# Scan layer of a four-layer network: two projection copies and the first output half moved in the hand-written plan

## Chip, cores and metric

One Trainium2 chip, one core. The metric is the device time of one execution in microseconds (us). The kernel before takes 3412.58 us, the median of 3 runs (3409.98 to 3416.41).

## The reference, cut to what matters

Four layers, each added to its input; the last one is a selective scan over 2304 tokens of each of three images, and the change touches nothing else.

```python
xz = jnp.einsum('blc,dc->bld', xn, in_proj_w)            # 256 -> 512 + 512 channels
x_in, z = jnp.split(xz, 2, axis=-1)
xc = jax.lax.conv_general_dilated(xc, conv_w, ...)       # 4 taps along the tokens
u = jax.nn.silu(xc).transpose(0, 2, 1)
x_dbl = jnp.einsum('bld,ed->ble', u, x_proj_w)           # -> dt_raw, B_ssm, C_ssm
dt = jax.nn.softplus(jnp.einsum('blr,dr->bld', dt_raw, dt_proj_w) + dt_proj_b)
def step(hst, inp):                                      # 512 channels x 16 states
    dA = jnp.exp(dt_t[:, :, None] * A)
    hst = hst * dA + dt_t[:, :, None] * B_t[:, None, :] * u_t[:, :, None]
    y_t = jnp.einsum('bdn,bn->bd', hst, C_t)
y = ys.transpose(1, 0, 2) + u * D_param
y = y * jax.nn.silu(z)
out = jnp.einsum('bld,cd->blc', y, out_proj_w)
```

All data are float32.

## The kernel before, in words

**Stages.** The first three layers (an attention block and two 3x3 convolutions) fill the first 2018 us. Then the scan layer runs for some 1370 us. Its tokens are cut into 18 chunks of 384 (3 images by 6), and a chunk's 512 inner channels into four blocks of 128 (m = 0 to 3; the change's "tiles"). One chunk holds 64 scan instructions on VectorE: four blocks, two halves of the states (h), eight parts. Scan n of a chunk is part n mod 8 of step (m, h), with n = 16m + 8h + part.

**A scan's feed.** ScalarE computes the decays of each scan, exp(dt A), into one of three PSUM banks (`decay`, L1792), VectorE scans them (`scan`, L1800). The decay for scan n + 3 is put out right behind scan n, since it takes scan n's bank. The scan works in place on a tile `hs`, which VectorE and GpSimd have filled with dt B u (`fill`): GpSimd the lower half (L1766, and a quarter at L1762), VectorE the upper (`fill_upper`, L1748), which reads `ps_r`. That is a two-bank PSUM tile, the only one of its pool; `spread_pe` (L1717) has TensorE write a quarter of dt u into each bank, once for each block m, at the end of its forerunner's first half. For the first half of a block (h = 0) `fill_upper` reads both banks; for the second half it reads the first bank only. After a step GpSimd multiplies by C (`times_c`, L1817), TensorE sums the states (`add_states`, L1829 and L1834) and VectorE gates with silu(z) (`gate`, L1841).

**What sets the order.** All else in a chunk is squeezed between these scans by a plan that is written by hand. A chunk has 16 places j (four scans each, so j = 0 to 3 is block 0), and in each the points BEGIN, MID, DONE, LATE (behind the first, second, third and fourth scan and the decay that follows it) and PE_ (for TensorE). An entry (j, point, rel, stage) runs `stage` for the chunk `rel` away from the one being scanned: rel 1 prepares the next chunk, rel -1 finishes the one before. `run` goes through `after`, `plan`, `gating` and `last_of_all` in this order. `keep_order` pins the resulting order on TensorE, VectorE, ScalarE and GpSimd, and each engine takes its instructions one after another; DMAs go through SyncE's queue in the order in which they are written.

**The stages around the change.** `project_x` (L1263) writes a block's projection into `whole[m % 2]`, one of two shared PSUM banks (`bank` is a view of these). `take_x` (L1269) copies it to SBUF on ScalarE. `taps` (L1273) makes the convolution, 4 matmuls into `bank[m % 2]`. `take_u` (L1281) moves that to `u` on ScalarE with the bias. `silu` (L1286) is one Silu over a whole chunk with a table load ahead of it, and another behind it (L229) that brings back the table with Exp. `silu(k.sz)` at (3, LATE) is that of z; `silu(k.u)` at (7, LATE) that of u. `project_y(k, mo)` (L1361, L1363) is half mo of the output projection with the residual, in `bank[mo]`; `store` copies it on ScalarE (L1373) and issues the output's DMA (L1374). `residual` (L1370) loads `k.ot`. Blocks 2 and 3 of the next chunk go through j = 2 to 5, the output half 0 of the chunk before through j = 5 and 6.

Of the kernel before, what the change touches and what calls it, by code (L numbers as in the profile page):

```python
# [16 lines left out]
P = 128  # L17
# [8 lines left out]
CH = 384  # L26
# [9 lines left out]
DI = 4  # L36
# [48 lines left out]
def net(  # L85
# [21 lines left out]
    nc = tc.nc  # L107
# [14 lines left out]
    def v(name, i=0, n=1):  # L122
        at = VEC_AT[name] + i
        return vec[:, at : at + n]

    ident = const.tile([P, P], F32, name="ident")
# [6 lines left out]
        out=gview, in_=gview, pattern=[[-8, 16], [0, 8]], compare_op=ALU.is_ge,  # L133
# [3 lines left out]
        out=gview, in_=gview, pattern=[[8, 16], [0, 8]], compare_op=ALU.is_ge,  # L137
# [243 lines left out]
    with ExitStack() as l0:  # L381
# [17 lines left out]
        def w(name, at, n):  # L399
            a = W0_AT[name] + at  # L400
            if a < W0_SPLIT:
                return w0a[:, a : a + n]
            return w0b[:, a - W0_SPLIT : a - W0_SPLIT + n]
# [14 lines left out]
        with ExitStack() as p1:  # L418
# [15 lines left out]
            for b in ORDER:  # L434
# [23 lines left out]
                for c in range(NCH):  # L458
                    for m, dst in ((0, y1), (1, cur[b])):
                        pm = ps.tile([P, 512], F32, tag="s", name="ps_y")  # L460
                        for ct in range(CT):
                            nc.tensor.matmul(  # L462
                                pm[:, :CH], ws[:, ct, m * P : (m + 1) * P], chunk(xb[:, ct, :], c),
                                start=ct == 0, stop=ct == CT - 1,
# [70 lines left out]
        with ExitStack() as p2:  # L535
# [9 lines left out]
            for i in range(NB):  # L545
# [400 lines left out]
                for mt in range(0, NT, 2):  # L946
                    pv = pair()
                    for j in range(2):
                        nc.tensor.matmul(
                            pv[:, j, :384], cur[2][:, (mt + j) * P : (mt + j + 1) * P], wn[2],  # L950
                            start=True, stop=True,
# [158 lines left out]
    def room(k, name):  # L1110
        return rooms[name][k.at % len(rooms[name])]
# [87 lines left out]

    class Chunk:  # L1200
        def __init__(self):
            self.second = {}


    whole = [psg.tile([P, 512], F32, name=f"ps_g{j}") for j in range(2)]
    bank = [t[:, :CH] for t in whole]
# [54 lines left out]
    def project_x(k, m):  # L1261
        for ct in range(CT):
            nc.tensor.matmul(  # L1263
                whole[m % 2][:, :XH], w3v["winx"][:, ct, m * P : (m + 1) * P], k.xn[:, ct, :],
                start=ct == 0, stop=ct == CT - 1,
            )

    def take_x(k, m):
        nc.scalar.copy(w3v["xi"][:, m % 3, :], whole[m % 2][:, :XH])  # L1269

    def taps(k, m):
        for tap in range(DCONV):
            nc.tensor.matmul(  # L1273
                bank[m % 2], w3v["taps"][:, m, tap, :], w3v["xi"][:, m % 3, tap : tap + CH],
                start=tap == 0, stop=tap == DCONV - 1,
            )

    def take_u(k, m):
        if m == 0:
            k.u = room(k, "u")  # L1280
        nc.scalar.activation(  # L1281
            k.u[:, m, :], bank[m % 2], AF.Identity, bias=v("conv_b", m)
        )

    def silu(t):
        nc.scalar.activation(t, t, AF.Silu)  # L1286
        exp_ln_tables()
# [68 lines left out]
            k.sz = room(k, "sz")  # L1356
        nc.scalar.copy(k.sz[:, m, :], bank[j])

    def project_y(k, mo, lo=0, hi=DI):
        if lo == 0:  # L1360
            nc.tensor.matmul(bank[mo], ident, k.ot[:, mo, :], start=True, stop=False)  # L1361
        for m in range(lo, hi):
            nc.tensor.matmul(  # L1363
                bank[mo], w("out", m * 256 + mo * P, P), k.sz[:, m, :],
                start=False, stop=m == DI - 1,
            )

# [2 lines left out]
        nc.sync.dma_start(k.ot, xd[k.b][:, :, k.c * CH : (k.c + 1) * CH])  # L1370

    def store(k, mo):
        nc.scalar.copy(k.ot[:, mo, :], bank[mo])  # L1373
        nc.sync.dma_start(  # L1374
            out[k.b, mo * P : (mo + 1) * P, k.c * CH : (k.c + 1) * CH], k.ot[:, mo, :]
        )
# [3 lines left out]
    BEGIN, MID, DONE, LATE, PE_ = range(5)  # L1380
# [15 lines left out]
        (2, DONE, 1, lambda k: project_x(k, 2)),  # L1396
        (2, LATE, 1, lambda k: take_u(k, 1)),
        (2, LATE, 1, lambda k: project_x(k, 3)),
        (3, LATE, 1, lambda k: take_x(k, 2)),
        (3, LATE, 1, lambda k: taps(k, 2)),  # L1400
        (4, BEGIN, 1, lambda k: take_x(k, 3)),
        (4, BEGIN, 1, lambda k: taps(k, 3)),
        (4, DONE, 1, lambda k: take_u(k, 2)),
        (5, MID, 1, lambda k: take_u(k, 3)),
        (7, LATE, 1, lambda k: silu(k.u)),
        (8, BEGIN, 1, project_u),
        (8, LATE, 1, take_dbc),
# [11 lines left out]
        (0, MID, 0, lambda k: k.at and take_z(k, 2, 0)),  # L1419
        (0, MID, 0, lambda k: k.at and take_z(k, 3, 1)),  # L1420
        (2, MID, -1, residual),
        (5, BEGIN, -1, lambda k: project_y(k, 0)),
        (6, MID, -1, lambda k: store(k, 0)),
        (7, PE_, -1, lambda k: project_y(k, 1)),
        (8, MID, -1, lambda k: store(k, 1)),
    ]

    last_of_all = [(3, LATE, 0, lambda k: silu(k.sz))]

# [246 lines left out]
    with ExitStack() as l3:  # L1676
# [35 lines left out]
        def spread_pe(k, m):  # L1712

            t = psr.tile([P, 2, 512], F32, name="ps_r")
            for q in range(2):
                r = slice(32 * q, 32 * q + 32)
                nc.tensor.matmul(  # L1717
                    t[:, q, :CH], rep[r].rearrange("p r d -> p (r d)"), k.dtu[r, m, :],
                    start=True, stop=True,
                )  # L1720
            k.ps = t


        steps = [(at, m, h) for at in range(len(todo)) for m in range(DI) for h in range(2)]
# [120 lines left out]
        k = chunks[0]  # L1845
        k.rows = {0: spread(k, 0)}
        spread_second(k, 0)
        spread_pe(k, 0)
        first_states(0)
        fill(0)  # L1850
        for n in range(3):
            decay(n)
        for s, (at, m, h) in enumerate(steps):
# [35 lines left out]
            if h == 0 and s + 2 < len(steps):  # L1889
                spread_pe(chunks[steps[s + 2][0]], steps[s + 2][1])  # L1890

        end = len(steps) - 1
        k = chunks[last]
        residual(k)
        for mo in range(2):
            project_y(k, mo, 0, DI - 1)
        add_states(end)
        gate(*steps[end][:2])
        for mo in range(2):
            project_y(k, mo, DI - 1, DI)  # L1900
            store(k, mo)
# [29 lines left out]
def net_kernel(tc, *args):  # L1931

    with tc.tile_pool(name="flag", bufs=1) as pool:
        flag = pool.tile([1, 1], I32, name="flag")
        net(tc, *args, flag, False)
        bad = tc.nc.values_load(flag[:1, :1])
        with tc.If(bad > 0):
            net(tc, *args, None, True)
# [77 lines left out]
```

## Time and profile before

| | |
|---|---|
| median of 3 runs | 3412.58 us (3409.98 to 3416.41) |
| the profiled execution's own time | 3411.51 us |
| its span, first to last instruction | 3409.8 us |
| scans, first start to last end | 2018.1 to 3389.4 us |
| one chunk (first scan to first scan), in turn | 77.4 and 76.3 us |
| VectorE busy in two chunks of 77.40 and 76.30 us | 73.83 and 73.72 us |
| ScalarE busy in them | 62.80 and 62.80 us |
| GpSimd busy in them | 72.30 and 69.73 us |
| TensorE busy in them | 64.08 and 61.84 us |
| VectorE's waits for a decay, all scans | 45.8 us in 50 waits, longest 1.4 us |

How to read it: the page has the busy time of each engine, the span in 40 slices, the chain that ended last and the costliest groups. A line names the kernel's line, the engine, the operation, what it writes `<-` reads, the shape, and the count; then busy time, mean ns of one and the idle time of its engine just ahead of it, with what ended that idle time. PE is TensorE, DVE VectorE, ACT ScalarE, POOL GpSimd, SP SyncE; PEclk is the TensorE clock that was granted, 1.00 being full. A timeline has start, duration, and in brackets the idle time ahead with its releaser; `x3` joins three instructions without a break. Times in it count from the span's start.

### The profile page before, as it was taken

What the parts mean: (1) busy time and instruction counts of PE and PEld (TensorE: products, weight loads), DVE (VectorE), ACT (ScalarE), POOL (GpSimd) and SP (SyncE); (2) the same over time, 40 slices, a digit from 0 to 9 for tenths busy, and PEclk for the clock granted to TensorE, in tenths of its full rate; (3) what the DMA queues carried; (4) which work ended last, traced back from release to release, by engine and by line L of the source; (5) the groups of instructions that cost most, each with busy time, mean ns of one, the idle gap of its engine ahead of it and who ended that gap; (6) DMA issues with size and microseconds to landing.
All of it is one profiled execution on the core that took longest, in us unless ns stands there. A gap on an engine that the chain in (4) does not pass through costs nothing.

```text
span 3409.8 us, 52160 instructions
## 1 busy us (share of the span) xinstructions
PE 3047.4 (89%) x19882; PEld 1442.5 (42%) x19882; DVE 2902.4 (85%) x3302; ACT 2381.6 (70%) x3596; POOL 1335.5 (39%) x457
## 2 busy tenths in 40 slices
PE   7999999999999999979999987878888888878785
PEld 4334343453333435547677753333333333333331
DVE  3799889959989996479966369999999999999998
ACT  2688888848888885332233558888888888888874
POOL 0000000000000000210000039999899999999897
PEclk8999999999999999989999998888889898988887
DMA  4000000010000002756501144545555454545552
GB/s 167 28 8 10 8 8 7 12 42 5 8 10 8 7 8 80 238 171 222 199 22 38 42 116 110 120 115 139 141 126 131 121 122 121 128 114 136 137 133 54
DMA packets 182152, 290.65 MB, mean 85 GB/s; under 512 B 34737, under 2 KB 148465, under 8 KB 179970
## 3 DMA queue, kind: packets, MB, share of 16 engines
q1 hardware_dynamic: 168658, 267.15, 29.0%
q10 hardware_dynamic: 13232, 20.06, 1.8%
q8 instruction: 158, 2.59, 0.3%
q14 instruction: 104, 0.85, 0.1%
HBM read 236.24 MB, written 50.64 MB: 84 GB/s over the span
## 4 chain that ended last, share of the span: by engine, by line
PE 59%; DVE 21%; ACT 11%; DMA 4%; issue 3%; POOL 1%; SPq 1%; ACTq 0%; DVEq 0%; POOLq 0%
PE ps_s L638 16%; PE acc L651 14%; DVE hs L1800 13%; PE ps_c L1533 8%; PE ps_g L1273 3%; PE ps_g L1222 3%; ACT ps_da L1792 2%; DVE u L296 2%; PE ps_y L462 2%; PE ps_m L665 1%; PE ps_s L1031 1%; PE ps_m L711 1%; PE ps_y L1834 1%; PE ps_g L1349 1%; ACT L229 1%
## 5 line engine op out<-in xcount | busy, mean ns | idle before, releaser
L642 ACT ACTIVATE pt<-ps_s 128x1024 f32<-128x1024 f32 x972 | 942.6, 1022 | 154.5 <-PE ps_s L638 141.8
L1800 DVE TENSOR_TENSOR_SCAN hs<-ps_da,hs 128x385 f32<-128x385 f32 x1152 | 1006.6, 940 | 47.4 <-ACT ps_da L1792 45.8
L857 DVE TENSOR_TENSOR part<-part,pt 128x2048 f32<-128x2048 f32 x396 | 906.8, 2290 | 41.2 <-ACT pt L642 18.4
L1792 ACT ACTIVATE ps_da<-dtr,u 128x384 f32<-128x384 f32 x1152 | 657.0, 583 | 201.7 <-DVE hs L1800 191.0
L164 POOL TENSOR_TENSOR rstd<-ve,mhalf 128x2 f32<-128x2 f32 (+1 forms) x26 | 16.4, 631 | 1476.5 <-DVE ve L162 1476.5
L638 PE MATMUL ps_s<-q,kt 32*128 32x512 f32 (+1 forms) x4320 | 576.4, 592 | 0.1
L651 PE MATMUL acc<-pt,vt 128*32 128x512 f32 (+1 forms) x4320 | 520.9, 561 | 0.2
L1533 PE MATMUL ps_c<-vt,u 128*128 128x288 f32 x1728 | 432.5, 411 | 21.0 <-DVE u L263 21.0
L1817 POOL TENSOR_TENSOR hc<-hs,x 128x3072 f32<-128x3072 f32 x72 | 405.3, 5629 | 5.4 <-DVE hs L1800 5.2
L1817 POOL TENSOR_TENSOR hc<-hs,bc 128x3072 f32<-128x3072 f32 x71 | 399.8, 5631 | 11.0 <-DVE hs L1800 7.9
L1533 PEld LDWEIGHTS ps_c<-vt,u 128*128 128x128 f32 x1728 | 331.0, 192 | 117.6 <-issue 19.8
L638 PEld LDWEIGHTS ps_s<-q,kt 32*128 32x128 f32 x4320 | 195.3, 183 | 199.1 <-issue 120.2
L1834 PE MATMUL ps_y<-hc,u 128*32 128x384 f32 x2304 | 252.0, 562 | 17.3 <-POOL hc L1817 17.3
L651 PEld LDWEIGHTS acc<-pt,vt 128*32 128x32 f32 x4320 | 94.4, 108 | 353.4 <-issue 326.7
L1273 PE MATMUL ps_g<-u 128*128 128x384 f32 x576 | 199.5, 494 | 21.0 <-ACT u L1269 20.9
L1766 POOL TENSOR_TENSOR hs<-dtur,x 128x1536 f32<-128x1536 f32 x72 | 209.2, 2905 | 7.2 <-DMA dtur<-dtud 7.2
L1766 POOL TENSOR_TENSOR hs<-dtur,bc 128x1536 f32<-128x1536 f32 x72 | 209.6, 2911 | 0.0
L1318 PE MATMUL ps_g<-wconv,u 17*128 17x384 f32 x144 | 79.2, 684 | 106.7 <-ACT x L1339 81.0
L1273 PEld LDWEIGHTS ps_g<-u 128*128 128x128 f32 x576 | 107.0, 190 | 110.5 <-ACT u L1269 42.2
L1222 PE MATMUL ps_g<-wconv,u 128*128 128x384 f32 x144 | 85.6, 765 | 64.6 <-ACT x L1339 64.1
L1834 PEld LDWEIGHTS ps_y<-hc,u 128*32 128x32 f32 x2304 | 65.4, 119 | 178.8 <-issue 152.6
L1549 ACT COPY cb<-ps_c 128x288 f32<-128x288 f32 x48 | 19.2, 399 | 158.4 <-PE ps_c L1533 144.2
(251 smaller groups left out, 3842.5 us busy)
## 6 DMA issues: line engine op xcount, KB each, us to landing
wconv<-in_we SPq DMA_DIRECT2D x144, 384.0 KB, 4.2
dtr<-dtd SPq DMA_DIRECT2D x288, 192.0 KB, 4.0
dtur<-dtud SPq DMA_DIRECT2D x288, 96.0 KB, 4.2
wconv<-xd SPq DMA_DIRECT2D x36, 384.0 KB, 4.9
x<-bcd SPq DMA_DIRECT2D x72, 192.0 KB, 5.3
dtd<-x SPq DMA_DIRECT2D x36, 384.0 KB, 3.5
dtuq<-dtud SPq DMA_DIRECT2D x288, 48.0 KB, 2.2
bc<-bcd SPq DMA_DIRECT2D x72, 192.0 KB, 5.1
```

What stands on the lines that cost most here:

```text
L638: nc.tensor.matmul(s[:, j, cols], kt[r, mt * P : (mt + 1) * P], q[r, :n], start=True, stop=True,)
L642: nc.scalar.activation(p[:, h0 : h0 + 2, :], s, AF.Exp)
L651: nc.tensor.matmul(acc[h * HD : (h + 1) * HD, :n], vt[:, mt, g * P + h * HD : g * P + (h + 1) * HD], p[:, h, cols], start=mt == 0, stop=mt ...
L857: ): nc.vector.tensor_tensor(part, first, p, ALU.add)
L1222: nc.tensor.matmul(bank[to], w3v["less"][:, int(to != ct), :], k.xg[:, ct, :], start=ct == 0, stop=ct == CT - 1,)
L1273: nc.tensor.matmul(bank[m % 2], w3v["taps"][:, m, tap, :], w3v["xi"][:, m % 3, tap : tap + CH], start=tap == 0, stop=tap == DCONV - 1,)
L1533: nc.tensor.matmul(pc[:, :HN], u[:, i, dy, ct, m * P : (m + 1) * P], vt[:, i, ct, dy * TW : dy * TW + HN], start=ct == 0 and dy == 0, stop ...
L1766: nc.gpsimd.tensor_tensor(states(s)[:, :, 2:4, 1:], chunks[at].rows[m][1].unsqueeze(1).broadcast_to([P, 2, 2, CH]), b_rows(s, 0, 2), ALU.mult,
L1792: nc.scalar.activation(slots[n % 3][:, 1 : CH + 1], chunks[at].rows[m][0][:, q, :], AF.Exp, scale=amat[:, col : col + 1],)
L1800: nc.vector.tensor_tensor_scan(b, slots[(8 * s + part) % 3][:, : CH + 1], b, 0.0, ALU.mult, ALU.add)
L1817: nc.gpsimd.tensor_tensor(hc, tiles[s][:, :, :, 1:], cb.broadcast_to([P, 2, 4, CH]), ALU.mult)
L1834: nc.tensor.matmul(k.y_ps[32 * q : 32 * q + 32, :CH], fold, hc[:, g, q, :], start=False, stop=h == 1 and g == 1,)
```

## The change

Blocks 2 and 3 are taken later: `take_x` and `taps` of block 2 go from (3, LATE) to (4, BEGIN), those of block 3 from (4, BEGIN) to (4, DONE); `take_u` from (4, DONE) and (5, MID) to (5, LATE) and (6, LATE). Output half 0 goes from (5, BEGIN) to (4, BEGIN), its `store` from (6, MID) to (5, DONE). So that it needs no shared bank there, it is summed in the second bank of `ps_r`, which `spread_pe` leaves in `lent`. The number of instructions of each engine is the same.

```diff
         def __init__(self):
-            self.second = {}
+            self.second, self.y_out = {}, {}
...
-    def project_y(k, mo, lo=0, hi=DI):
+    def project_y(k, mo, lo=0, hi=DI, into=None):
         if lo == 0:
-            nc.tensor.matmul(bank[mo], ident, k.ot[:, mo, :], start=True, stop=False)
+            k.y_out[mo] = bank[mo] if into is None else into
+            nc.tensor.matmul(k.y_out[mo], ident, k.ot[:, mo, :], start=True, stop=False)
         for m in range(lo, hi):
             nc.tensor.matmul(
-                bank[mo], w("out", m * 256 + mo * P, P), k.sz[:, m, :],
+                k.y_out[mo], w("out", m * 256 + mo * P, P), k.sz[:, m, :],
                 start=False, stop=m == DI - 1,
             )
...
     def store(k, mo):
-        nc.scalar.copy(k.ot[:, mo, :], bank[mo])
+        nc.scalar.copy(k.ot[:, mo, :], k.y_out[mo])
...
-        (3, LATE, 1, lambda k: take_x(k, 2)),
-        (3, LATE, 1, lambda k: taps(k, 2)),
-        (4, BEGIN, 1, lambda k: take_x(k, 3)),
-        (4, BEGIN, 1, lambda k: taps(k, 3)),
-        (4, DONE, 1, lambda k: take_u(k, 2)),
-        (5, MID, 1, lambda k: take_u(k, 3)),
+        (4, BEGIN, 1, lambda k: take_x(k, 2)),
+        (4, BEGIN, 1, lambda k: taps(k, 2)),
+        (4, DONE, 1, lambda k: take_x(k, 3)),
+        (4, DONE, 1, lambda k: taps(k, 3)),
+        (5, LATE, 1, lambda k: take_u(k, 2)),
+        (6, LATE, 1, lambda k: take_u(k, 3)),
...
-        (5, BEGIN, -1, lambda k: project_y(k, 0)),
-        (6, MID, -1, lambda k: store(k, 0)),
+        (4, BEGIN, -1, lambda k: project_y(k, 0, 0, DI, lent[0])),
+        (5, DONE, -1, lambda k: store(k, 0)),
...
+    lent = [None]
...
             k.ps = t
+            lent[0] = t[:, 1, :CH]
```

## The prediction

> **What bounds the kernel now.** I read the page's groups first: the scans are VectorE's largest group, they come one after another over 1371 us, and little idle time stands ahead of them.
>
> ```profile
> L1800 DVE TENSOR_TENSOR_SCAN hs<-ps_da,hs 128x385 f32<-128x385 f32 x1152 | 1006.6, 940 | 47.4 <-ACT ps_da L1792 45.8
> ```
>
> So VectorE bounds the scan layer, and time can be won only where it waits. The view of waits, for VectorE over the scan layer, has one entry of weight, the same 45.8 us:
>
> ```profile
> DVE hs L1800 <- ACT ps_da L1792: 45.8, 50, 1.4
> ```
>
> Sorted by the scan that waits, this is 17 waits at scan 19 of a chunk (18.7 us; 1.13 us in most chunks), 16 at scan 59 (14.0 us; 1.37 and about 0.35 us in turn), 16 at scan 61 (12.2 us) and one more. The change lies around scan 19. The timeline of ScalarE in the chunk that starts at 2480.70 shows how that wait arises:
>
> ```profile
> 2494.90 0.59 ACT L1792 ACTIVATE ps_da<-dtr,u 128x384 f32<-128x384 f32 x1 [0.27 <-DVE hs L1800]
> 2496.22 0.48 ACT L1269 COPY u<-ps_g 128x387 f32<-128x387 f32 x1 [0.74 <-PE ps_g L1263]
> 2496.72 1.28 ACT L1286 ACT_TABLE_LOAD   x1
> ...
> 2500.92 0.58 ACT L1792 ACTIVATE ps_da<-dtr,u 128x384 f32<-128x384 f32 x1
> 2501.44 0.47 ACT L1269 COPY u<-ps_g 128x387 f32<-128x387 f32 x1
> ```
>
> After the decay for scan 18, ScalarE idles 0.74 us for TensorE's projection of block 2, copies it, and only then starts z's Silu. The decay for scan 19 starts at 2500.92. VectorE in the same stretch (the scan's second line is scan 19):
>
> ```profile
> 2494.77 0.54 DVE L1841 TENSOR_TENSOR sz<-ps_y,sz 128x384 f32<-128x384 f32 x1
> ...
> 2497.75 2.66 DVE L1800 TENSOR_TENSOR_SCAN hs<-ps_da,hs 128x385 f32<-128x385 f32 x3
> 2501.53 4.47 DVE L1800 TENSOR_TENSOR_SCAN hs<-ps_da,hs 128x385 f32<-128x385 f32 x5 [1.13 <-ACT ps_da L1792]
> 2505.92 0.54 DVE L1748 TENSOR_TENSOR hs<-ps_r,x 128x384 f32<-128x384 f32 x1
> 2506.37 1.80 DVE L1800 TENSOR_TENSOR_SCAN hs<-ps_da,hs 128x385 f32<-128x385 f32 x2
> ```
>
> The last chunk has no next one to prepare, so it has z's Silu without the copies. ScalarE there, then VectorE:
>
> ```profile
> 3337.86 1.28 ACT L1286 ACT_TABLE_LOAD   x1
> ...
> 3341.95 2.28 ACT L1792 ACTIVATE ps_da<-dtr,u 128x384 f32<-128x384 f32 x4
> ```
>
> ```profile
> 3337.13 0.54 DVE L1841 TENSOR_TENSOR x<-ps_y,x 128x384 f32<-128x384 f32 x1
> ...
> 3340.11 6.91 DVE L1800 TENSOR_TENSOR_SCAN hs<-ps_da,hs 128x385 f32<-128x385 f32 x8
> 3346.92 0.54 DVE L1748 TENSOR_TENSOR hs<-ps_r,bc 128x384 f32<-128x384 f32 x1
> ```
>
> Eight scans, no break: z's Silu alone just fits. Counted from the gate (L1841), the table load starts at 0.73 instead of 1.95, and the fill (L1748) comes at 9.79 instead of 11.15.
>
> [...] Here ScalarE's store and VectorE's fill read different banks of one tile[...]; but in the built order of the changed kernel the fill of a block's second half, which waited for no other engine, now has a wait on ScalarE, whose count is that of the store's copy. No run shows its cost yet. [...] PEclk is 0.50 or 1.00, its pieces are multiples of 3.413 us, and two chunk periods, 77.36 and 76.28 us, make 153.6, or 45 such windows.
>
> **The change part by part.** All times below count from the gate.
>
> 1. *block 2's copy behind the Silu.* The burst starts at 0.73, as in the last chunk. Its length from load to the next small copy is 2500.81 - 2496.72 = 4.09, the small copy (L1782) takes 0.11 to the next start, the decay 0.58: decay 19 is ready at 5.51. Scan 19 is due at 2.98 + 2.57 = 5.55. The wait of 1.13 goes, with 0.1 that scan 20 lost.
> 2. *The two copies after it.* Starts follow each other by 0.52 (decay to copy), 0.38 (copy to decay), 0.51 (decay to decay): copy of block 2 at 5.45, decays 20 and 21 at 5.83 and 6.34, copy of block 3 at 6.85, decays 22 and 23 at 7.23 and 7.74, decay 24 at 8.35. Each is ready before its scan, scan 20 perhaps 0.04 late. Their cover is the three decays of lead and the two `take_u` that stood here and leave.
> 3. *The added wait.* Decay 25 can't start before scan 22 has freed its bank: scan 22 starts at 8.14, and decays start 0.97 after such a start, so 9.11. The store's copy follows at 9.62, takes 0.47, and VectorE answers 0.03 later: fill at 10.12. It was due at 9.84, so VectorE waits 0.28, with scans 24 to 27 behind it and GpSimd's product after them. The next scan starts at 10.57; before, 2506.37 - 2494.77 = 11.60. Gain 1.03 per chunk. Bounds for the wait: 0.28 is the least if ScalarE keeps pace; 0.8 if it is one copy late.
> 4. *TensorE.* The order is a permutation of the same matmuls: sums of block 0 (2.17 from 2.55 on), output half 0 (3.32, to 8.04), `taps` of blocks 2 and 3 (2.6 each, to 13.4). The store wants its result at 9.62: 1.5 to spare. `take_u` of block 2 waits to 10.7, some 0.2, hidden because decay 27 can't start before 11.54. `k.ot` landed 5 us into the chunk, 12 us before its use. The second bank is free: VectorE's last read of it ends at 3.1, and the output half starts at 4.72. The next `spread_pe` comes after output and copy anyway.
> 5. *Queues.* SyncE holds at the store until ScalarE's copy; that end moves from 14.4 to 10.1, so the loads behind it (L1709, L1701) start earlier. On GpSimd nothing moves. In the two chunks that I followed, its fills were ready at least 1.7 us before VectorE's scans wanted them; 1.03 of that goes.
>
> Sum: 16 chunks by 1.03 is 16.5; the first has 0.79 + 0.11 to gain and no store, 0.9; the last has only the new wait, -0.28. Together 17.1.
>
> 6. *The clock.* The wait at scan 59 hangs on eight matmuls (L1222) that meet a cold or warm TensorE. In two chunks, the second window after their start:
>
> ```profile
> 2544.90:2548.40 3.50, 2.11 (x4) 0.66 (x2) 2.80 (x4) 2.21 (x6) 3.50 (x2) 0.68 1.06 295
> 2622.20:2625.60 3.40, 1.95 (x7) 0.91 (x6) 3.01 (x5) 3.10 (x7) 3.40 (x2) 0.99 1.07 295
> ```
>
> Still mostly half clock: wait 1.37; full clock: 0.3. Mean now 0.87. Without this wait a chunk takes 75.98, after the change 74.95, and 22 windows are 75.09. With the small wait the period is 75.25, and a chunk moves against the grid by only 0.16; with the large one by 1.2. It should stay longer where the wait is small: I estimate a mean of 0.55, 0.32 by 16 = 5 more. Ends: 0.25 in every chunk, +9.9; 1.37, -8.0.
>
> The profiled execution, 3411.5, becomes 3411.5 - 22.1 = 3389.4. The median is 1.1 above it: 3390.5, say 3391.
>
> **Rivals.**
> - *Clock unlucky*: part 6 at its bad end, 3412.6 - 17.1 + 8.0 = 3403.5. For it: each chunk takes the large wait today in every second chunk; against: it can't lock there with steps of 1.2. 0.15.
> - *The wait takes the place*: the copy comes late by one more copy and decay each time, the wait is 1.0 instead of 0.28: 17 by 0.72 = 12 less, 3403. For it: three instructions of ScalarE follow each other there without a gap. Against: it still idles 0.2 ahead of decay 25. 0.12.
> - *Nothing gained*: Silu and decay 19 still stall, since the margin at scan 19 is 0.04: 3412. Against: the last chunk. 0.05.
> - *Slower*: VectorE now waits on ScalarE's copy and so on TensorE's output half. If that ends 2.6 later than 8.04, the fill comes at 11.15 and all is lost; with the clock at half from 2.55 on, it ends at 13.5, the fill comes at 14.0, and a chunk loses 2.9: 17 by 2.9 = 49, 3462. Against: the granted clock in this stretch (the 1.00), in each chunk that I looked at. 0.10.
>
> ```profile
> 2497.30:2510.30 13.00, 13.00 (x65) 6.16 (x63) 11.87 (x15) 11.84 (x22) 13.00 (x4) 1.00 0.20 46
> ```
>
> **How the numbers follow.** The forecast has 0.58. The range goes from the good end of the clock (3385.5, and 4 for what isn't costed) to both middle rivals with 3 more: 3381 to 3406. It leaves out the last two rivals, 0.15. A measurement tells 0.2% (7 us) from none: faster 0.85, within 0.05, slower 0.10.
>
> **What would show it.** Right: no VectorE wait at scan 19; a new one, near 0.3 by 17, at the fill of a block's second half with ScalarE's store as releaser; Silu's load right behind a decay; scans 59 and 61 still waiting, periods of 75 to 76. Wrong: that fill's wait over 1 us, with TensorE's output half as the store's releaser, or GpSimd ahead of scans.

## The result and the profile after

The changed kernel takes 3394.84 us, the median of 5 runs (3390.85 to 3397.77), against 3412.58 us (5 runs): a ratio of 0.9948, 95% interval 0.9933 to 0.9962. That is 17.7 us less; forecast were 21.6 less, 3391 us, with a range of 3381 to 3406. The profiled execution took 3393.68 us with a span of 3391.9 us.

The scans (now L1803) still lead VectorE's groups on the page; the wait for decays (now L1795) has gone from 45.8 to 25.9 us:

```profile
L1803 DVE TENSOR_TENSOR_SCAN hs<-ps_da,hs 128x385 f32<-128x385 f32 x1152 | 1004.6, 937 | 27.5 <-ACT ps_da L1795 25.9
```

In the view of waits, for VectorE in the scan layer, a new line stands below it. It is the wait that the prediction announced, the fill (L1751) for the store's copy (L1374):

```profile
DVE hs L1803 <- ACT ps_da L1795: 25.9, 34, 1.8
DVE hs L1751 <- ACT wconv L1374: 3.6, 17, 0.2
```

The timeline of the same chunk as before, which now starts at 2473.80, ScalarE first:

```profile
2487.99 0.58 ACT L1795 ACTIVATE ps_da<-dtr,u 128x384 f32<-128x384 f32 x1 [0.27 <-DVE hs L1803]
2488.60 1.28 ACT L1286 ACT_TABLE_LOAD   x1
...
2492.80 0.58 ACT L1795 ACTIVATE ps_da<-dtr,u 128x384 f32<-128x384 f32 x1
2493.32 0.48 ACT L1269 COPY u<-ps_g 128x387 f32<-128x387 f32 x1
...
2497.07 0.58 ACT L1795 ACTIVATE ps_da<-dtr,u 128x384 f32<-128x384 f32 x1 [0.26 <-DVE hs L1803]
2497.59 0.47 ACT L1374 COPY wconv<-ps_r 128x384 f32<-128x384 f32 x1
2497.96 0.58 ACT L1795 ACTIVATE ps_da<-dtr,u 128x384 f32<-128x384 f32 x1
2498.70 0.58 ACT L1281 ACTIVATE u<-ps_g,vec 128x384 f32<-128x384 f32 x1 [0.16 <-PE ps_g L1273]
```

The table load comes right behind the decay for scan 18, and the copy of block 2 behind the decay for scan 19. VectorE:

```profile
2487.88 0.53 DVE L1844 TENSOR_TENSOR sz<-ps_y,sz 128x384 f32<-128x384 f32 x1
...
2490.86 7.02 DVE L1803 TENSOR_TENSOR_SCAN hs<-ps_da,hs 128x385 f32<-128x385 f32 x8
2498.09 0.56 DVE L1751 TENSOR_TENSOR hs<-ps_r,x 128x384 f32<-128x384 f32 x1 [0.21 <-ACT wconv L1374]
2498.57 1.80 DVE L1803 TENSOR_TENSOR_SCAN hs<-ps_da,hs 128x385 f32<-128x385 f32 x2
```

Eight scans run without a break, as they did in the last chunk of the kernel before. From the gate to scan 24 it is 2498.57 - 2487.88 = 10.69 us; before it was 11.60.

**Where the 17.8 us between the two profiled executions come from.** From the first scan's start to the last one's, 1370.3 us before are 1354.3 now, 16.1 less; some 2 us fell ahead of the scan layer, where the program is the same (its first scan started between 2014.6 and 2027.4 us in the profiles below, so that part is chance). Of the 16.1: a chunk without its wait at scan 59 takes 75.06 instead of 75.98 us in most, which makes 14.6 in 16 chunks; the waits at scan 59 fell from 14.0 to 11.3 us, 2.7; the first chunk, its wait at scan 59 apart, is 1.1 longer; and the last chunk is the same within 0.1, since its 0.21 us at the fill took the place of a wait of 0.21 at scan 44.

### The profile page after: what moved, and what is told of

Same layout as the page of the kernel before. It is cut to its first block, busy times and chain, and to the rows that moved or that the text cites. A ratio compares the mean times of both kernels' runs of the same rounds, so it can differ in the third digit from the quotient of the medians.

```text
span 3391.9 us, 52176 instructions
## 1 busy us (share of the span) xinstructions
PE 3034.7 (89%) x19882; PEld 1442.9 (43%) x19882; DVE 2902.7 (86%) x3302; ACT 2379.2 (70%) x3596; POOL 1334.7 (39%) x457
## 4 chain that ended last, share of the span: by engine, by line
PE 54%; DVE 30%; ACT 8%; issue 4%; DMA 3%; POOL 0%; SPq 0%; DVEq 0%; ACTq 0%; POOLq 0%
DVE hs L1803 19%; PE ps_s L638 16%; PE acc L651 14%; PE ps_c L1535 8%; DVE hs L1751 3%; PE ps_g L1222 2%; PE ps_s L1031 2%; ACT ps_da L1795 2%; DVE u L296 2%; PE ps_y L462 2%; PE ps_m L665 2%; PE ps_m L711 1%; PE acc L529 1%; PE ps_s L518 1%; DVE ps_g L1334 1%
## 5 line engine op out<-in xcount | busy, mean ns | idle before, releaser
L1803 DVE TENSOR_TENSOR_SCAN hs<-ps_da,hs 128x385 f32<-128x385 f32 x1152 | 1004.6, 937 | 27.5 <-ACT ps_da L1795 25.9
L1795 ACT ACTIVATE ps_da<-dtr,u 128x384 f32<-128x384 f32 x1152 | 656.7, 582 | 196.0 <-DVE hs L1803 187.5
L1318 PE MATMUL ps_g<-wconv,u 17*128 17x384 f32 x144 | 79.4, 685 | 112.5 <-ACT x L1339 87.0
L1222 PE MATMUL ps_g<-wconv,u 128*128 128x384 f32 x144 | 82.9, 745 | 62.9 <-ACT x L1339 62.4
```

Of the source, the lines that this page charges most:

```text
L1222: nc.tensor.matmul(bank[to], w3v["less"][:, int(to != ct), :], k.xg[:, ct, :], start=ct == 0, stop=ct == CT - 1,)
L1795: nc.scalar.activation(slots[n % 3][:, 1 : CH + 1], chunks[at].rows[m][0][:, q, :], AF.Exp, scale=amat[:, col : col + 1],)
L1803: nc.vector.tensor_tensor_scan(b, slots[(8 * s + part) % 3][:, : CH + 1], b, 0.0, ALU.mult, ALU.add)
```

## The experiments

Each kernel was timed beside the kernel before, 4 to 6 runs of each and 20 of the half alone. A ratio is to the kernel before in the same rounds, where its medians were 3412.6 to 3413.5 us; the last kernel ran on another chip than the seven above it. Waits and periods are from one profile of each kernel. "Scan stretch" is from the first scan's start to the last one's in the profile, which leaves out the chance ahead of it. A clock window is here a stretch of 3.413 us, and the grid is their row: in the traces of the kernel before and the changed one the granted clock reads 0.50 or 1.00, each of its pieces lasts a whole number of times 3.413 us (in the changed kernel's scan layer 1 to 17), and 22 times 3.413 is 75.09.

| kernel | median us | ratio, 95% interval | scan stretch us | waits per chunk at scans 19 to 22 and fill; at 59; at 61 |
|---|---|---|---|---|
| before | 3412.58 | | 1370.3 | 1.13; 1.37 or 0.3 in turn; 0.75 |
| changed | 3394.84 | 0.9948 [0.9933, 0.9962] | 1354.3 | 0.21; 0.14 to 1.38; 0.75 |
| copy alone | 3425.25 | 1.0034 [1.0021, 1.0047] | 1380.4 | 1.64; 0.12 to 1.38; 0.75 |
| half alone | 3418.68 | 1.0014 [1.0008, 1.0021] | 1376.5 | 1.34; 0.11 to 1.37; 0.75 |
| no second bank | 3401.43 | 0.9966 [0.9953, 0.9979] | 1359.8 | 0, but 0.62 at scan 35; 0.22 to 1.38; 0.75 |
| store a scan earlier | 3386.77 | 0.9925 [0.9913, 0.9938] | 1344.4 | 0; 0.31 to 0.42; 0.75 |
| and copy a scan later | 3388.35 | 0.9923 [0.9911, 0.9935] | 1344.0 | 0; 0.32 to 0.59; 0.75 |
| TensorE kept busy | 3385.39 | 0.9924 [0.9907, 0.9940] | 1344.4 | 0.21; 0; 0.75, three chunks 1.6 to 2.2 |
| all three | 3383.22 | 0.9919 [0.9906, 0.9932] | 1343.2 | 0; 0; 0.75, every third chunk 2.1 |
| all three, busy longer | 3380.87 | 0.9908 [0.9891, 0.9924] | 1336.7 | 0; 0; 0.86 |

(At scan 59 the first three chunks of the runs from "store a scan earlier" on are left out, in which the periods settle.)

### The copy alone

The change's own idea without what surrounds it: block 2's copy behind the Silu, but `take_u` and the output half left where they were.

```diff
-        (4, DONE, 1, lambda k: take_x(k, 3)),
-        (4, DONE, 1, lambda k: taps(k, 3)),
-        (5, LATE, 1, lambda k: take_u(k, 2)),
-        (6, LATE, 1, lambda k: take_u(k, 3)),
+        (4, BEGIN, 1, lambda k: take_x(k, 3)),
+        (4, BEGIN, 1, lambda k: taps(k, 3)),
+        (4, DONE, 1, lambda k: take_u(k, 2)),
+        (5, MID, 1, lambda k: take_u(k, 3)),
...
-        (4, BEGIN, -1, lambda k: project_y(k, 0, 0, DI, lent[0])),
-        (5, DONE, -1, lambda k: store(k, 0)),
+        (5, BEGIN, -1, lambda k: project_y(k, 0)),
+        (6, MID, -1, lambda k: store(k, 0)),
```

> One part alone: the copies and taps of blocks 2 and 3 both at (4, BEGIN), all else as in the kernel before (take_u at (4, DONE) and (5, MID), output half 0 in its shared bank at (5, BEGIN)). Theory: the wait at scan 19 is gone, but the wait moves on: taps of block 2 start only when the copy is there, so take_u of block 2 at (4, DONE) holds ScalarE and the decay of scan 22 until TensorE is done. I expect no wait at scan 19, some 0.4 us at scan 20 and 1.2 us at scan 22 of each chunk, and a time of 3410 to 3420 us, no gain on the kernel before. Rival, that the copy's place is all that counts and the other moves are dressing: 3391 to 3396 us, as the changed kernel.

Measured: 3425.25 us, slower than before. The timeline of this kernel, VectorE, then the place on ScalarE that causes the second wait:

```profile
2509.48 3.51 DVE L1803 TENSOR_TENSOR_SCAN hs<-ps_da,hs 128x385 f32<-128x385 f32 x4
2513.38 1.81 DVE L1803 TENSOR_TENSOR_SCAN hs<-ps_da,hs 128x385 f32<-128x385 f32 x2 [0.38 <-ACT ps_da L1795]
2516.44 1.81 DVE L1803 TENSOR_TENSOR_SCAN hs<-ps_da,hs 128x385 f32<-128x385 f32 x2 [1.26 <-ACT ps_da L1795]
```

```profile
2515.36 0.58 ACT L1281 ACTIVATE u<-ps_g,vec 128x384 f32<-128x384 f32 x1 [1.57 <-PE ps_g L1273]
```

Scan 19 has no wait any more; scans 20 and 22 wait 0.38 and 1.26 instead, more than the 1.13 that went. ScalarE idles 1.57 us ahead of `take_u`, because the taps start only after the moved copy. So the later `take_u` is no dressing: without it the wait only changes its place. The time is 5 us above the range that I expected, though both waits were as expected: my range did not follow from them. Waits of 1.64 instead of 1.13 make 8.2 us in 16 chunks, and the first chunk is 1.8 longer, together the 10.0 us by which the scan stretch grew.

### The output half alone

```diff
-        (4, BEGIN, 1, lambda k: take_x(k, 2)),
-        (4, BEGIN, 1, lambda k: taps(k, 2)),
-        (4, DONE, 1, lambda k: take_x(k, 3)),
-        (4, DONE, 1, lambda k: taps(k, 3)),
-        (5, LATE, 1, lambda k: take_u(k, 2)),
+        (3, LATE, 1, lambda k: take_x(k, 2)),
+        (3, LATE, 1, lambda k: taps(k, 2)),
+        (4, BEGIN, 1, lambda k: take_x(k, 3)),
+        (4, BEGIN, 1, lambda k: taps(k, 3)),
+        (4, DONE, 1, lambda k: take_u(k, 2)),
```

> The other part alone: output half 0 in the second bank at (4, BEGIN), its store at (5, DONE), take_u of block 3 at (6, LATE) so that it doesn't wait for TensorE; the copies and taps stay where the kernel before has them. Theory: the wait of 1.13 us at scan 19 stays, and the fill of a block's second half gets its wait for the store, 0.2 to 0.3 us by 17; 3412 to 3420 us. Rival, that the gain comes from the earlier output half (its bank free sooner, SyncE's queue released sooner): 3400 us or less.

Measured: 3418.68 us, 0.14% slower. VectorE's timeline has the old wait and the new one one after the other:

```profile
2500.97 4.47 DVE L1803 TENSOR_TENSOR_SCAN hs<-ps_da,hs 128x385 f32<-128x385 f32 x5 [1.13 <-ACT ps_da L1795]
2505.65 0.56 DVE L1751 TENSOR_TENSOR hs<-ps_r,x 128x384 f32<-128x384 f32 x1 [0.21 <-ACT wconv L1374]
```

So the early output half brings nothing by itself; it costs the fill's wait. A chunk without its wait at scan 59 takes 76.28 instead of 75.98 us, 0.30 more (why an idle gap of 0.21 costs 0.30 comes below, where the store moves). This kernel came into the expected range and far from the rival's 3400.

### Without the second bank

```diff
-        (4, BEGIN, -1, lambda k: project_y(k, 0, 0, DI, lent[0])),
-        (5, DONE, -1, lambda k: store(k, 0)),
+        (6, BEGIN, -1, lambda k: project_y(k, 0)),
+        (7, MID, -1, lambda k: store(k, 0)),
```

> The changed kernel without the lent bank: output half 0 later, in its shared bank at (6, BEGIN), its store at (7, MID). Theory: the second bank isn't what wins the time; without it the fill's wait of 0.21 us goes, and nothing else changes but a late store right ahead of u's Silu, which may cost up to 0.1 us at scan 35. With 0.21 less, a chunk without the wait at scan 59 is 74.85 us, which is 0.24 short of 22 clock windows (75.09): the wait at scan 59 should settle at 0.2 to 0.3 in every chunk instead of running from 0.15 to 1.37, and the time should fall by 17 times 0.21 and 16 times 0.45, to 3384 us. Rival 1, the second bank is what makes it: slower than the changed kernel, over 3398 us. Rival 2, the clock's grid plays no part: 3391 us, with waits at scan 59 as varied as before.

Measured: 3401.43 us, so the expectation of 3384 us failed, although the fill's wait is gone as expected; the number is that of the first rival, over 3398. ScalarE ahead of u's Silu, and VectorE's scan 35:

```profile
2510.22 0.48 ACT L1374 COPY wconv<-ps_g 128x384 f32<-128x384 f32 x1 [0.94 <-PE ps_g L1364]
2510.59 1.09 ACT L1795 ACTIVATE ps_da<-dtr,u 128x384 f32<-128x384 f32 x2
2511.71 1.28 ACT L1286 ACT_TABLE_LOAD   x1
```

```profile
2516.52 1.81 DVE L1803 TENSOR_TENSOR_SCAN hs<-ps_da,hs 128x385 f32<-128x385 f32 x2 [0.62 <-ACT ps_da L1795]
```

The store waits 0.94 us for TensorE's output half and pushes the other Silu back; scan 35 pays 0.62 in 16 chunks, 9.7 us. I had allowed 0.1 for it. What the second bank is good for is this: the output half gets done before u's Silu, whose stretch has no more room than that of z's. Another place for it in the shared bank was not tried.

### The store one scan earlier

```diff
-        (5, DONE, -1, lambda k: store(k, 0)),
+        (5, MID, -1, lambda k: store(k, 0)),
```

> The changed kernel with the store of output half 0 one scan earlier, at (5, MID). Theory: the fill waits for this copy only because it stands behind decay 25; behind decay 24 it ends 0.85 us sooner, and TensorE has the half ready at 22.3 us of the chunk, when ScalarE wants it at about 22.9. So the fill's wait goes from 0.21 to 0, a chunk without the wait at scan 59 is 74.85 us, the period locks at 22 clock windows, 75.09, with 0.2 to 0.3 us at scan 59 in every chunk: 3384 us. Rival, no lock: the fill's wait goes and nothing else, 3391 us. Rival, the fill's wait is for something else than the copy: 3395 us.

Measured: 3386.77 us. VectorE has no wait at the fill, and at scans 59 and 61 of a late chunk it shows:

```profile
2493.61 0.53 DVE L1751 TENSOR_TENSOR hs<-ps_r,x 128x384 f32<-128x384 f32 x1
```

```profile
2986.36 1.81 DVE L1803 TENSOR_TENSOR_SCAN hs<-ps_da,hs 128x385 f32<-128x385 f32 x2 [0.38 <-ACT ps_da L1795]
2988.91 0.96 DVE L1803 TENSOR_TENSOR_SCAN hs<-ps_da,hs 128x385 f32<-128x385 f32 x1 [0.75 <-ACT ps_da L1795]
```

The fill's wait was for the copy, then, and for nothing else. And the lock came as expected, too. The median does not show it, since the five runs, 3382.7 to 3390.9 us, take in 3384 and nearly the rival's 3391; the periods do. From the eleventh chunk on the periods are 75.03 to 75.13 us, on average the 75.09 of 22 clock windows, with 0.31 to 0.38 at scan 59. A chunk without that wait got 0.31 us shorter, to 74.75, not 0.21: a scan's start overlaps its forerunner's end by 0.09 (a scan of 0.94 every 0.85), so an idle gap of 0.21 is a start that is 0.3 late. Of the 9.8 us by which the scan stretch is shorter than the changed kernel's (8 in the medians), 16 by 0.32 is 5.1; the rest is the wait at scan 59, 6.6 us in all instead of 11.3.

### And the copy one scan later

```diff
-        (4, BEGIN, 1, lambda k: take_x(k, 2)),
-        (4, BEGIN, 1, lambda k: taps(k, 2)),
+        (4, MID, 1, lambda k: take_x(k, 2)),
+        (4, MID, 1, lambda k: taps(k, 2)),
-        (5, DONE, -1, lambda k: store(k, 0)),
+        (5, MID, -1, lambda k: store(k, 0)),
```

> The store at (5, MID), and the copy and taps of block 2 one scan later, at (4, MID), behind the decay of scan 20. Theory: scan 20 loses the 0.1 us by which it starts late in the changed kernel, so a chunk without the wait at scan 59 is some 74.65 us instead of 74.75. The clock's grid takes it back: the period stays at 22 windows, 75.09 to 75.10, and the wait at scan 59 grows from 0.35 to about 0.45 in every chunk; the time is that of the kernel with the store alone, 3387 us within 2. Rival, the lock was chance: 1.7 us faster, with the wait at scan 59 as before.

Measured: 3388.35 us, as expected no faster. Waits at scan 59 are 0.43 in most chunks, and the period is 75.06 in most, with one of 75.2 now and then, on average 75.09 from the third chunk to the sixteenth. The 0.1 us that this edit saved between scan 19 and scan 59 came back at scan 59.

### TensorE kept busy ahead of L1222

```diff
+    def keep_warm(k):
+        for _ in range(4):
+            nc.tensor.matmul(lent[0], ident, k.u[:, 3, :], start=True, stop=True)
...
+        (12, BEGIN, 0, keep_warm),
```

> The changed kernel and four matmuls more per chunk, at (12, BEGIN), whose result nobody reads (identity by u into the second bank of ps_r): they fill TensorE's idle time of 3.9 us ahead of the eight matmuls of L1222. Theory: the waits at scan 59, 0.15 to 1.37 us, come from TensorE at half clock in these eight; with TensorE busy up to them the clock is full, the waits fall below 0.2 in nearly all chunks, and the time falls by about 16 times 0.6, to 3385 us. Rival, the wait is not the clock's: waits unchanged and 3395 us, or more by what the added matmuls delay.

Measured: 3385.39 us. TensorE in a late chunk, the added matmuls and then L1222, and VectorE, where the five scans 56 to 60 are in one piece. The trace has two records for each of these float32 matmuls (20026 on the page instead of 19882, 144 more for 72 in the code), so four in the code are eight here; the first line shows six of the eight added ones, since the view opens at 2978:

```profile
2977.83 2.10 PE L1383 MATMUL ps_r<-x,ident 128*128 128x384 f32 x6
2980.59 2.85 PE L1222 MATMUL ps_g<-wconv,u 128*128 128x384 f32 x8 [0.66 <-ACT x L1339]
```

```profile
2984.13 4.40 DVE L1808 TENSOR_TENSOR_SCAN hs<-ps_da,hs 128x385 f32<-128x385 f32 x5
2989.28 0.96 DVE L1808 TENSOR_TENSOR_SCAN hs<-ps_da,hs 128x385 f32<-128x385 f32 x1 [0.75 <-ACT ps_da L1800]
```

L1222 takes 2.85 us instead of 4.3 to 5.5, and the wait at scan 59 is gone in all chunks. In the changed kernel it takes 5.49 us at 2381.15, where the granted clock is 0.50, and at 1865.88, ahead of the scan layer, 2.85 at 1.00. So these waits are the clock's: more work on TensorE, and less time. Most periods are 75.00, below 75.09, but this does not take the kernel off the grid: each chunk starts 0.09 us earlier against the windows, until in the twelfth scan 61 waits 2.17 us instead of 0.75, and the periods of the fourth to the sixteenth chunk average 75.09 again.

### All three, and all three with TensorE busy for longer

The first has the store at (5, MID), the copy at (4, MID) and five added matmuls; the second also has three behind L1222.

```diff
+    def keep_warm(k, n):
+        for _ in range(n):
+            nc.tensor.matmul(lent[0], ident, k.u[:, 3, :], start=True, stop=True)
...
+        (12, BEGIN, 0, lambda k: keep_warm(k, 5)),
+        (13, PE_, 0, lambda k: keep_warm(k, 3)),
```

> Store at (5, MID), copy of block 2 at (4, MID), and five such matmuls at (12, BEGIN). Theory: with no wait at scan 59 to give, the period is free of the clock's grid and both savings count: 74.65 to 74.75 us a chunk, 3378 to 3381 us. Rival, something else holds the period at 75.09 (GpSimd, whose work in a chunk is 72 us, or the DMAs): 3387 us.

> Store at (5, MID), copy of block 2 at (4, MID), five unread matmuls at (12, BEGIN) as in the run before, and three more at (13, PE_), between L1222 and L1229. In the run before, the wait at scan 59 is gone, but in a third of the chunks scan 61 waits 2.12 us instead of 0.75, where the clock falls to half some 5 us after L1222's start. Theory: that window holds the 1.45 us in which TensorE waits for ScalarE ahead of L1229; filled, the clock stays full, scan 61 waits 0.75 in all chunks, and the period is 74.57 throughout: six times 1.37 less, 3375 us within 3. Rival, the added matmuls delay L1229 itself by what they take: scan 61 waits longer in every chunk, 3385 us or more.

Measured: 3383.22 and 3380.87 us, so both missed what was expected, 3378 to 3381 and 3375 within 3. In the first, periods are 74.57 us, a little under the expected 74.65, but in about every third chunk 75.94. TensorE in such a chunk, and scan 61:

```profile
3129.26 2.85 PE L1222 MATMUL ps_g<-wconv,u 128*128 128x384 f32 x8 [0.87 <-ACT x L1339]
3134.76 2.93 PE L1229 MATMUL ps_g<-wconv,mean 128*128 128x384 f32 x4 [2.65 <-ACT wconv L1237]
```

```profile
3139.31 0.96 DVE L1808 TENSOR_TENSOR_SCAN hs<-ps_da,hs 128x385 f32<-128x385 f32 x1 [2.12 <-ACT ps_da L1800]
```

The idle stretch has moved to the place behind the fast L1222 (2.65 us), and in these chunks L1229 behind it takes 2.93 us instead of 1.56, near twice as long, as L1222 does at clock 0.50 (5.49 against 2.85). So what was saved came back at scan 61: counted from behind one slow chunk to behind a later one (chunks 8 to 15, three of them slow), eight periods take 600.7 us, 75.09 each. The rival, that something holds the period at 75.09, was right in this; it is not GpSimd or the DMAs, which it named, but, by the time of L1229, again the clock. It goes with this that the four kernels from "store a scan earlier" to "all three" have the same scan stretch within 1.2 us. With three matmuls in that gap the second kernel leaves the grid: its periods are 74.65 to 74.69 from the second chunk to the sixteenth, and scan 61 waits 0.86 (0.91 at most), where 0.1 more than the 0.75 is what I put down to the added matmuls ahead of L1229. Its scan stretch is 6.5 us shorter, as against 8 expected; 2.6 were lost in the seventeenth chunk, where ScalarE waits 3.46 us for TensorE's L1349, which stands behind the added matmuls. The median fell by 2.4 only, within what the stretch ahead of the scans adds by chance. Against the changed kernel it is 17.6 us less in the scan stretch, and the fastest of all here.

## Why the prediction was right, point by point

1. *Block 2's copy behind the Silu*: right. The load starts 0.72 after the gate (0.73 forecast), the decay for scan 19 at 4.92 (4.93, the forecast end of 5.51 less 0.58), and the wait is gone in all chunks but the first, which keeps 0.37.
2. *The copies after it*: the term that was too small. I gave scan 20 a delay of 0.04; scans 19 and 20 start 0.95 apart instead of 0.85, so it is 0.10, as before the change. That is most of the difference between 1.03 a chunk and the 0.92 measured.
3. *The added wait*: right in place, cause and size. The fill starts at 10.21, with the 0.1 of the second point in it, against 10.12 forecast; scan 23's start plus 0.85 gives 9.92, so it is 0.29 late (0.28 forecast). The store a scan earlier showed that nothing else is behind it. The copy reads one bank and the fill the other; what they share is the tile. No run had the two banks as two tiles, but the last kernel has such a wait a second time: there TensorE's added matmuls, which write the second bank, wait for a fill that reads the first one only:

```profile
2981.60 2.20 PE L1383 MATMUL ps_r<-x,ident 128*128 128x384 f32 x6 [0.58 <-DVE hs L1757]
```

4. *TensorE*: right. The output half ended at 8.2 after the gate (2493.34 + 2.74 - 2487.88), the store wanted it at 9.71. `take_u` waited 0.16 for the taps (0.2 forecast), and VectorE lost nothing by it.
5. *Queues*: right; the store's DMA is issued 10.2 us after the gate (2498.09), before 14.4, and VectorE gets no new wait on a DMA or on GpSimd.
6. *The clock*: the mechanism is right, its size not. I put the mean wait at scan 59 at 0.55, and it is 0.70 (11.3 in 16). The period without it being 75.06, only 0.03 short of 22 windows, the wait has to be 0.03 for the period to stay; it never gets below 0.14. So each chunk falls back against the grid, first slowly, then by 1.3, and in five chunks it comes round. Five successive chunks, the first two columns being stretch and length:

```profile
2397.70:2473.80 76.10, 63.35 (x266) 28.30 (x265) 73.65 (x90) 61.87 (x115) 70.76 (x21) 0.89 0.53 127
2473.80:2549.50 75.70, 61.88 (x266) 27.83 (x265) 73.82 (x91) 62.70 (x123) 70.68 (x21) 0.89 0.53 129
2549.50:2624.90 75.40, 61.57 (x266) 27.64 (x265) 73.81 (x91) 62.70 (x123) 70.63 (x21) 0.91 0.54 129
2624.90:2700.10 75.20, 61.38 (x266) 27.57 (x265) 73.76 (x91) 62.63 (x123) 71.00 (x21) 0.91 0.53 130
2700.10:2776.50 76.40, 62.53 (x266) 27.87 (x265) 73.75 (x90) 62.69 (x123) 71.90 (x21) 0.89 0.53 127
```

Together 378.8 us, and 111 windows of 3.413 are 378.9. VectorE's busy time (the third of the engines' columns) is the same within 0.2 in all five; only the waiting differs.

7. *The sum*: 17.1 for the moves became 13.4 (14.6 in 16 chunks, less 1.1 in the first), 5 for the clock 2.7, and chance ahead of the scans gave 2, so that luck brought the profiled time closer to the forecast than the terms were. The last chunk was to lose 0.28 and lost nothing. The first is the other term that failed: instead of gaining 0.9 it is 1.1 longer. Most of that is chance as well: its waits at scans 14 and 15, ahead of all that the change moves, are 2.2 instead of 1.0. In the ten profiles here these two waits make 0.95 to 1.12 us in five (the kernel before is one of them), and 2.0 to 2.5 in the other five (the changed kernel is one). In the kernel before the granted clock rises to 1.00 10.2 us into that chunk, in the changed one 12.9. The change's own gain there, from scan 16 to scan 24, is 0.43, because scan 19 still waits 0.37.

The rivals: "the clock unlucky" did not come, nor did "the wait takes the place", "nothing gained" or "slower"; the output half ended at 8.2 in the chunk shown, far from the 10.64 at which all would have been lost, and no copy of it waited for TensorE.

## What to carry to other kernels

Where one engine feeds the engine that bounds, count the lead (here three decays) against the longest burst that is put in front of it, and keep out of the burst whatever else waits for a third engine; but follow what is moved to its own consumer, or the wait only changes its place. When a second user borrows part of a tile, look for the wait that it adds to the first user, even on another bank (0.21 us at each fill here), and put the borrower's read where the owner comes well after it. And where the loop waits for matmuls that the trace shows at half clock, look at TensorE's idle gaps ahead of them, and at all of them: here 0.1 us that was saved came back as waiting, with the period at 75.09 us; added matmuls in the first gap brought L1222 from 4.3 to 5.5 us down to 2.85 but, with the other savings, moved the waiting to scan 61 (2.12 us instead of 0.75 in about every third chunk), and with the second gap filled as well the periods were 74.65 to 74.69.

## What the runs showed of the hardware that was not expected

**0.1 us of start time.** In the changed kernel L1222 starts at 2305.94 us in one chunk and at 2381.15 in the next, 0.54 and 0.64 us into a window that has clock 0.50. These windows, with TensorE's busy time first, the granted clock third from the end, and each followed by the window after it:

```profile
2305.40:2308.80 3.40, 2.86 (x5) 1.65 (x6) 3.40 (x5) 3.06 (x8) 0.15 (x1) 0.50 0.95 236
2308.85:2312.20 3.35, 1.91 (x7) 0.89 (x6) 3.28 (x5) 2.95 (x8) 3.35 (x2) 1.00 1.08 247
2380.55:2383.90 3.35, 2.75 (x5) 1.54 (x6) 3.35 (x5) 3.01 (x8) 1.17 (x2) 0.50 1.08 255
2384.00:2387.30 3.30, 2.63 (x5) 0.88 (x3) 3.30 (x5) 1.75 (x5) 3.30 (x2) 0.50 1.07 276
```

Behind the first window the clock is 1.00, behind the third 0.50: 0.1 us of start time goes with 3.4 us of full clock, and with 1.2 us at scan 59 (0.14 against 1.38). In the scan layers of the kernel before and the changed one, L1222 starts in a window at clock 0.50 29 times: 11 times up to 0.54 us into it, and the next window has 1.00; 18 times 0.62 us or more into it, and the next has 0.50. TensorE's busy time in the window alone does not tell them apart: behind the third window, with 2.75 us, the clock is 0.50, behind the fourth, with 2.63 us in the 3.30 shown, it is 1.00. What decides was not shown.

The round of five goes with this. In the changed kernel the wait at scan 59 falls from 0.42 us, where L1222 starts 0.09 ahead of a window, over 0.25 (0.31 into one) to 0.14, where it starts 0.54 into one, and then jumps to 1.38. By these waits a chunk that starts 0.1 us later waits some 0.05 us less. That this is what holds the period with the store a scan earlier is my estimate from them.

**Busy and still at half clock.** In 16 of the changed kernel's 17 chunks with L1318, matmuls over 17 rows, a window at clock 0.50 that TensorE filled with the last of them and the matmuls after it was followed by another at 0.50; here is one:

```profile
3052.90:3056.30 3.40, 3.40 (x6) 0.50 0.77 220
3056.40:3059.80 3.40, 3.38 (x18) 0.51 1.02 207
```

The first is all L1318 and the start of L1832, busy for 3.40 us of 3.40, and the next has 0.51. Whether it is the number of rows was not tried apart.
